# Where the first feed-forward block of a gated cross-attention kernel is normalized, quantized and transposed

## The chip, the cores and the metric

The kernel runs on one core of one Trainium2 chip. The metric is the device time of one execution in microseconds. A difference below about 0.3% (2.2 us here) can't be told from no change.

The core has five engines that each work through a queue of their own, in order: TensorE (PE; its weight loads are shown apart as PEld), VectorE (DVE), ScalarE (ACT), GpSimd (POOL) and SyncE (SP, which issues most of the DMA transfers). An engine stops at an instruction whose inputs aren't ready, and everything behind it in its queue stops too.

## The reference

4096 rows `x` of width 512 (two batches of 2048) go through a layer norm, 16-head attention over 77 context rows, a gated residual, a second layer norm, and a feed-forward net with per-tensor 8-bit quantization:

```
x = x + tanh(g_xattn) * attn(layernorm(x), ctx)        # 16 heads of 32, float32
h = layernorm(x)                                        # 4096 x 512
xq = round(h / sx),  sx = max|h| / 127                  # one scale for the whole tensor
h = gelu((xq @ w1q.T + b1) * sw1 * sx)                  # 4096 x 2048
hq = round(h / sh),  sh = max|h| / 127                  # one scale again
x = x + tanh(g_ffn) * ((hq @ w2q.T + b2) * sw2 * sh)
```

Each scale is a maximum over the whole tensor. Nothing of the first product can start before the last row of the attention is known, and nothing of the second before the last row of the GELU.

## The kernel before, in words

The rows are cut in 8 blocks (`i`) of 512 (`TB`), each held in SBUF as `X[i]`, four tiles (`t`) of 128 rows.

**Attention.** For every block there are eight steps `s` (head group `s // 2`, half of the rows `s % 2`), written out by hand. VectorE's and TensorE's orders are taken as written, where `tc.issue_after(ins)` queues an instruction behind `ins` on its engine and the other engines' orders come from a scheduler. A step holds a `softmax` (scores on TensorE, maximum and subtraction on VectorE, exponential on ScalarE, sum `sm` and reciprocal `rs` on VectorE, product with `rs` on GpSimd, line 282), the transposes `pta` of its result to `aT` (`transpose_a`), the product with the values (`apply_v`: `pc`, copied to `cT`) and the output projection of the block before (`project_o`, line 324, which adds to `X[i]`). `aT` has three buffers, `cT` seven. After its output projection a block gets the statistics of the second layer norm (`norm2_stats`: `mean2`, `rstd2`; the power that makes `rstd2` is a GpSimd instruction, line 142) and the block's largest absolute normalized value (`norm2_max`: `xf`, `tm`, `xmax`, lines 338 to 350). For the last block this is done tile by tile behind each `project_o(NB - 1, t)`.

**Between the stages.** `normalize_x(0, nc.gpsimd)` writes the normalized first block to `xs0` on GpSimd (line 520, four instructions), under a high priority and behind the last softmax product on GpSimd. `scale_of(xmax, "x", ...)` makes `m_x`, a TensorE product that spreads the maximum over the partitions (`pg_x`, line 153), and `s_x`, `inv_x`. `quantize_x(0, xs, 1)` quantizes the block tile by tile (VectorE for tiles 0 and 1, ScalarE and VectorE for 2 and 3), transposes each tile on TensorE (`px`, line 544) and copies it to `xqT` on ScalarE (line 547).

**First product.** For each block `i`, 128 matmuls of 128x512 (`ph`, line 574; eight of them fill one of two PSUM tiles), the GELU on ScalarE (line 581, two for each PSUM tile) into one of eight `G` buffers, a maximum of it on VectorE (`hmax`, line 591) and a store of `G` to DRAM (line 602). While block `i` is multiplied, block `i + 1` is prepared on VectorE: four normalizations (`xs`, line 520), two instructions that quantize the whole block (lines 164 and 165, to `xq`), and four copies (line 549) of the transposes `px` that TensorE makes between its matmuls. `xs`, `xq` and `xqT` have two buffers each (`fwork`), and `px` two PSUM buffers. In

```python
            if i + 1 < NB:
                with tc.issue_after(last):
                    xs = normalize_x(i + 1, nc.vector)
                xqT, last = quantize_x(i + 1, xs, NT)
```

`last` is the last quantizing instruction of the block before, and each block renews it. Within these bounds the scheduler picks the order.

**Second product.** Its scale needs the last `hmax`. The two last blocks' `G` are still in SBUF; the others are read back from DRAM.

Of the kernel before, what the change touches and what calls it, by code (L numbers as in the profile page):

```python
# [8 lines left out]
F32 = mybir.dt.float32  # L9
BF16 = mybir.dt.bfloat16  # L10
AF = mybir.ActivationFunctionType
ALU = mybir.AluOpType
# [3 lines left out]
P = 128  # L16
# [23 lines left out]
def tile_flamingo_gated_block(  # L40
# [47 lines left out]
    wq_sb = awts.tile([P, KC, D], F32, name="wq_sb")  # L88
    wo_sb = awts.tile([P, KC, D], F32, name="wo_sb")
    ctx_sb = awts.tile([P, B, KC, NK], F32, name="ctx_sb")  # L90
    bv_sb = awts.tile([NK, D], F32, name="bv_sb")
    bq_sb = const.tile([P, KC], F32, name="bq_sb")
    bk_sb = const.tile([P, KC], F32, name="bk_sb")
    tg = const.tile([P, 2], F32, name="tg")
    bo_sb = const.tile([P, D], F32, name="bo_sb")
    b1_sb = const.tile([P, FC], F32, name="b1_sb")
    b2_sb = const.tile([P, D], F32, name="b2_sb")

    load_x(0, pieces=NT)
    nc.scalar.dma_start(bq_sb, bq)  # L100
# [11 lines left out]
    nc.sync.dma_start(tg[:, 1:2], g_ffn.to_broadcast([P, 1]))  # L112
    nc.sync.dma_start(bo_sb, bo.to_broadcast([P, D]))
    nc.sync.dma_start(b1_sb, b1)
    nc.sync.dma_start(b2_sb, b2.to_broadcast([P, D]))

    ident = const.tile([P, P], F32, name="ident")
    make_identity(nc, ident)
# [5 lines left out]
    nc.gpsimd.memset(mhalf, -0.5)  # L124

    w1q = const.tile([P, KC, FF], BF16, name="w1q")
    w2q = const.tile([P, FC, D], BF16, name="w2q")
    mean2 = const.tile([P, NB, NT, 2], F32, name="mean2")
    rstd2 = const.tile([P, NB, NT], F32, name="rstd2")
# [15 lines left out]
    def scale_of(maxima, name, psum, tag):  # L145
# [13 lines left out]
        nc.vector.reciprocal(inv, s)  # L159
        return s, inv  # L160

    def quantize(dst, src, inv):

        nc.vector.tensor_scalar(src, src, inv, MAGIC, ALU.mult, ALU.add)
        return nc.vector.tensor_scalar(dst, src, MAGIC, None, ALU.subtract).ins
# [3 lines left out]

    s_w, inv_w = {}, {}  # L170
    with actx:
        work = actx.enter_context(tc.tile_pool(name="work", bufs=2))
        ps_s = actx.enter_context(tc.tile_pool(name="ps_s", bufs=2, space=PSUM))
        ps_t = actx.enter_context(tc.tile_pool(name="ps_t", bufs=2, space=PSUM))
        ps_p = actx.enter_context(tc.tile_pool(name="ps_p", bufs=2, space=PSUM))

        kblk, vblk = [], []
        for b in range(B):
            kb = awts.tile([P, NG, GK], F32, name=f"kb{b}")
            nc.gpsimd.memset(kb, 0.0)  # L180
            kblk.append(kb)
            vblk.append(awts.tile([NK, D], F32, name=f"vb{b}"))

        def project_k(b, g):

# [147 lines left out]
        def norm2_max(i, t0=0, t1=NT):  # L333

            tm = small.tile([P, NT], F32, tag="tm", name=f"tm{i}_{t0}")
            for t in range(t0, t1):
                xn = work.tile([P, D], F32, tag="xn", name=f"xf{i}_{t}")
                nc.vector.tensor_scalar(
                    xn,
                    X[i][:, t, :],  # L340
                    mean2[:, i, t, 0:1],
                    rstd2[:, i, t : t + 1],
                    ALU.subtract,
                    ALU.mult,
                )
                nc.vector.tensor_reduce(
                    tm[:, t - t0 : t - t0 + 1], xn, AX.X, ALU.max, apply_absolute_value=True
                )
            k = i if t1 - t0 == NT else NB - 1 + t0
            nc.vector.tensor_reduce(xmax[:, k : k + 1], tm[:, : t1 - t0], AX.X, ALU.max)  # L350

# [63 lines left out]
            project_k(0, 1)  # L417
        softmax(0, 0)
        for i in range(NB):
            for s in range(2 * NG):  # L420
                last = None
                if s + 1 < 2 * NG:
                    last = softmax(i, s + 1)
                    last_product = last["POOL"]
                elif i + 1 < NB:
                    last = softmax(i + 1, 0)
                transpose_a(i, s, 0)

                if i == 0 and s < 2:
                    project_k(0, s + 2)  # L430
                if s == 0:
                    if i > 0:
                        apply_v(i - 1, NG - 1)
                    project_q(i, 1)
                if i == 0 and s == 1:
                    project_v(0)
                if i == 0 and s == 2:


                    with tc.issue_after(last["ACT"]):  # L440
                        nc.scalar.activation(tg, tg, AF.Tanh)
                    with tc.issue_after(last["POOL"]):
                        nc.gpsimd.tensor_scalar(bo_sb, bo_sb, tg[:, 0:1], None, ALU.mult)
                if s in (2, 4):
                    project_q(i, 1 + s // 2)
                    apply_v(i, s // 2 - 1)
                if s in (1, 3, 5, 6) and i > 0:
                    project_o(i - 1, (1, 3, 5, 6).index(s))
                if s == 6:
                    apply_v(i, 2)  # L450
                if i + 1 < NB:
                    if s == 3:
                        with tc.issue_after(last["DVE"]):
                            norm(i + 1)
                    if s in (5, 6):
                        for t in (2 * s - 10, 2 * s - 9):
                            transpose_x(i + 1, t)
                transpose_a(i, s, 1)
                if s == 6 and i + 1 < NB:
                    project_q(i + 1, 0)  # L460
                if i == 0 and 3 <= s < 7:
                    for b in range(1, B):
                        project_k(b, s - 3)
                        if s == 6:
                            project_v(b)
                if s == 7 and i > 0:
                    norm2_stats(i - 1)
                    norm2_max(i - 1)
                if last is not None:
                    with tc.issue_after(last["DVE"]):  # L470
                        weight_step(i, s)
                    t = s - NT if i == 0 else s // 2
                    if t >= 0 and (i == 0 or s % 2 == 0):
                        with tc.issue_after(last["POOL"]):
                            add_bias(i, t)
            if i + 2 < NB:
                load_x(i + 2)
            if i == 0:
                load_w("w1", w1_piece, range(4))
            if i == 2:  # L480
                load_w("w2", w2_piece, range(2))
# [4 lines left out]
        for t in range(NT):  # L486
            project_o(NB - 1, t)
            last = norm2_stats(NB - 1, t, t + 1)
            if t > 0:
                with tc.issue_after(last):  # L490
                    norm2_max(NB - 1, t - 1, t)
        norm2_max(NB - 1, NT - 1, NT)
    s_w1, s_w2 = s_w["w1"], s_w["w2"]


# [1 line left out]
    hidden_dram = ctx.enter_context(  # L497
        tc.tile_pool(name="hidden_dram", bufs=1, space=bass.MemoryType.DRAM)
    )

    def gtile(name):
        return gpool.tile([P, GF, TB], F32, tag="G", name=name)
# [5 lines left out]
    with ExitStack() as fctx:  # L508
# [5 lines left out]
            tc.tile_pool(name="ps_x", bufs=2, space=PSUM, reuse_waits="tile")  # L514
        )

        def normalize_x(i, engine):
            xs = fwork.tile([P, NT, D], F32, tag="xs", name=f"xs{i}")
            for t in range(NT):
                engine.tensor_scalar(  # L520
                    xs[:, t, :],
                    X[i][:, t, :],
                    mean2[:, i, t, 0:1],
                    rstd2[:, i, t : t + 1],
                    ALU.subtract,
                    ALU.mult,
                )
            return xs

        def quantize_x(i, xs, n):  # L530

            xq = fwork.tile([P, NT, D], BF16, tag="xq", name=f"xq{i}")
            xqT = fwork.tile([P, KC, TB], BF16, tag="xqT", name=f"xqT{i}")
            for t0 in range(0, NT, n):
                v, vq = xs[:, t0 : t0 + n, :], xq[:, t0 : t0 + n, :]
                if n == 1 and t0 >= NT // 2:
                    nc.scalar.activation(v, v, AF.Copy, bias=MAGIC, scale=inv_x)
                    last = nc.vector.tensor_scalar(vq, v, MAGIC, None, ALU.subtract).ins
                else:
                    last = quantize(vq, v, inv_x)  # L540
                for t in range(t0, t0 + n):
                    px = ps_x.tile([P, KC, P], BF16, tag="px", name=f"px{i}_{t}")
                    for kc in range(KC):
                        nc.tensor.transpose(px[:, kc, :], xq[:, t, kc * P : (kc + 1) * P], identb)  # L544
                    dst = xqT[:, :, t * P : (t + 1) * P]
                    if n == 1:
                        nc.scalar.copy(dst, px)  # L547
                    else:
                        nc.vector.tensor_copy(dst, px)
            return xqT, last  # L550


        with tc.issue_after(last_product), tc.high_priority(offset=300):
            xs = normalize_x(0, nc.gpsimd)
        s_x, inv_x = scale_of(xmax, "x", ps_g, "pg")
        xqT, last = quantize_x(0, xs, 1)
        s1 = const.tile([P, 1], F32, name="s1")
        nc.vector.tensor_tensor(s1, s_x, s_w1, ALU.mult)
        b1s = const.tile([P, FC], F32, name="b1s")
        nc.vector.tensor_scalar(b1s, b1_sb, s1, None, ALU.mult)  # L560
        for i in range(NB):
            cur = xqT
            if i + 1 < NB:
                with tc.issue_after(last):
                    xs = normalize_x(i + 1, nc.vector)
                xqT, last = quantize_x(i + 1, xs, NT)
            for a in range(GT):
                G = gtile(f"G{i}_{a}")
                for v in range(GF // 2):
# [149 lines left out]
```

## Time and profile before

| | |
|---|---|
| median of 14 executions | 728.15 us (722.54 to 732.19) |
| the profiled execution: its time, its span | 730.5 us, 728.6 us |
| busy: PE, DVE, ACT, POOL | 672.2, 525.9, 346.0, 212.0 us |
| attention | 0 to 450.8 us |
| from the last `po` to the first `ph` | 450.8 to 467.3 us |
| first product | 467.3 to 596.0 us |
| second product | 600.9 us to the end |
| first product: PE busy, DVE busy | 127.4, 109.6 of 128.75 us |

The times are microseconds from the span's start. A row of the timeline gives the start, the time until the last of a merged group ended, the engine, the line of the kernel, the operation, the tile written and read, shapes, the count, and in brackets the engine's idle time just ahead and what ended it. The profile's busy time of PE contains modelled ends of matmuls, so a busy PE may still lose time.

### The profile page before, as it was taken

Reading aid. Unit: us, or ns where it says so; the run is one execution under the profiler, and the core shown is the slowest. Engines: PE = TensorE matmul, PEld = TensorE weight load, DVE = VectorE, ACT = ScalarE, POOL = GpSimd, SP = SyncE. Lnnn points to the kernel's source line nnn. Section 1 sums busy time; section 2 is a strip of 40 time slices with the busy share of each in tenths; the row PEclk is TensorE's granted clock in tenths of the full one; section 3 lists DMA queues with packets and bytes.
Section 4 is the critical chain, followed back from the end, with each engine's and each line's share of the span. In section 5 each row is a group of like instructions: output and inputs, shape, how many; then the busy total and the mean of one; then the engine's idle time right before and its main releaser. Section 6 shows DMA issues by size and latency. Waiting matters only on the chain.

```text
span 728.6 us, 7864 instructions
## 1 busy us (share of the span) xinstructions
PE 672.2 (92%) x2881; PEld 333.9 (46%) x2904; DVE 525.9 (72%) x821; ACT 346.0 (47%) x474; POOL 212.0 (29%) x164
## 2 busy tenths in 40 slices
PE   4998999899999999999999997499999978999977
PEld 2654545445445454554555543244444433444432
DVE  3564688879888889587577567699997769855442
ACT  1454444344343334444444441377777779454540
POOL 3223333234232342432333234100000009992000
PEclk9999999999999999999999999599999998999999
DMA  9801200021311311100000000057666107698861
GB/s 304 328 0 50 66 1 1 13 93 68 116 58 58 116 58 58 58 1 1 0 1 1 0 1 0 0 231 288 253 268 274 73 0 289 241 385 304 307 249 72
DMA packets 26430, 85.40 MB, mean 117 GB/s; under 512 B 3531, under 2 KB 3531, under 8 KB 20248
## 3 DMA queue, kind: packets, MB, share of 16 engines
q1 hardware_dynamic: 24520, 83.54, 30.9%
q10 hardware_dynamic: 1872, 1.37, 0.6%
q8 instruction: 23, 0.38, 0.2%
q14 instruction: 15, 0.12, 0.1%
HBM read 51.34 MB, written 33.55 MB: 117 GB/s over the span
## 4 chain that ended last, share of the span: by engine, by line
PE 66%; DVE 12%; DMA 7%; POOL 6%; ACT 6%; issue 2%; SPq 0%; POOLq 0%; DVEq 0%; ACTq 0%
PE ph L574 16%; PE pq L245 12%; PE po L317 11%; PE pf L636 8%; PE pta L295 7%; PE ps L261 6%; DMA Gb<-h 6%; POOL e L282 4%; PE pc L304 3%; DVE mx L270 2%; DVE sm L279 2%; ACT Gb L627 1%; DVE e L274 1%; POOL xs L520 1%; PE px L544 1%
## 5 line engine op out<-in xcount | busy, mean ns | idle before, releaser
L282 POOL TENSOR_TENSOR e<-e,rs 128x616 f32<-128x616 f32 x64 | 78.0, 1219 | 269.9 <-DVE rs L281 198.6
L574 PE MATMUL ph<-xqT,w1q 128*128 128x512 bf16 x499 | 124.0, 384 | 1.9 <-ACT xqT L547 0.7
L636 PE MATMUL pf<-w2q,hq 128*128 128x512 bf16 x502 | 114.7, 388 | 10.6 <-DVE hq L628 6.3
L245 PE MATMUL pq<-xnT,wq_sb 128*128 128x512 f32 x256 | 120.3, 609 | 0.9 <-ACT xnT L237 0.9
L296 ACT COPY aT<-pta 77x512 f32<-77x512 f32 x128 | 73.4, 580 | 98.6 <-PE pta L295 98.4
L317 PE MATMUL po<-wo_sb,cT 128*128 128x512 f32 x256 | 116.4, 593 | 0.0
L581 ACT ACTIVATE G<-ph,b1s,s 128x512 f32<-128x512 f32 x128 | 99.5, 777 | 30.1 <-PE ph L574 24.6
L650 POOL TENSOR_TENSOR x<-x,b_sb 128x512 f32<-128x512 f32 x32 | 58.9, 1879 | 142.2 <-DVE b_sb L607 142.2
L295 PEld LDWEIGHTS pta<-ident,e 128*77 128x77 f32 x512 | 60.3, 149 | 69.2 <-POOL e L282 34.0
L295 PE MATMUL pta<-ident,e 128*77 128x128 f32 x512 | 79.9, 282 | 12.3 <-POOL e L282 9.8
L591 DVE TENSOR_REDUCE hmax<-G 128x1 f32<-128x1024 f32 (+1 forms) x65 | 75.2, 1197 | 16.4 <-ACT G L581 16.1
L636 PEld LDWEIGHTS <-hq 128*128 128x128 bf16 x512 | 50.5, 99 | 74.5 <-issue 8.8
L270 DVE TENSOR_REDUCE mx<-ps 128x8 f32<-128x616 f32 x64 | 50.4, 788 | 44.8 <-PE ps L261 44.8
L574 PEld LDWEIGHTS <-w1q 128*128 128x128 bf16 x512 | 49.5, 98 | 68.5 <-issue 19.6
L261 PE MATMUL ps<-kb,qT 128*128 128x308 f32 x256 | 79.3, 430 | 0.5 <-ACT kb L200 0.4
L245 PEld LDWEIGHTS pq<-xnT,wq_sb 128*128 128x128 f32 x256 | 46.9, 194 | 52.7 <-issue 49.2
L627 ACT ACTIVATE Gb<-Gb,inv_h 128x2048 f32<-128x2048 f32 x24 | 47.6, 1999 | 47.8 <-DMA Gb<-h 47.8
L279 DVE TENSOR_REDUCE sm<-e 128x8 f32<-128x616 f32 x64 | 50.5, 789 | 26.8 <-ACT e L277 26.4
L277 ACT ACTIVATE e<-e 128x616 f32<-128x616 f32 x64 | 45.8, 716 | 50.0 <-DVE e L274 45.7
L317 PEld LDWEIGHTS po<-wo_sb,cT 128*128 128x128 f32 x256 | 46.4, 190 | 45.6 <-issue 43.9
L628 DVE TENSOR_SCALAR hq<-Gb 128x2048 bf16<-128x2048 f32 x24 | 36.5, 1531 | 32.9 <-ACT Gb L627 32.9
L274 DVE TENSOR_TENSOR e<-ps,mx 128x616 f32<-128x616 f32 x64 | 51.0, 796 | 3.3 <-POOL e L282 0.5
(90 smaller groups left out, 622.6 us busy)
## 6 DMA issues: line engine op xcount, KB each, us to landing
h<-G SPq DMA_DIRECT2D x24, 1024.0 KB, 3.9
Gb<-h SPq DMA_DIRECT2D x24, 1024.0 KB, 7.9
raw_w<-in_w2T SPq DMA_DIRECT2D x8, 1024.0 KB, 5.2
out_y<-x SPq DMA_DIRECT2D x32, 256.0 KB, 3.5
x<-in_x SPq DMA_DIRECT2D x7, 1024.0 KB, 5.3
raw_w<-in_w1T SPq DMA_DIRECT2D x4, 1024.0 KB, 10.0
x<-in_x SPq DMA_DIRECT2D x4, 256.0 KB, 5.5
wq_sb<-in_wqT ACTq DMA_DIRECT2D x1, 1024.0 KB, 10.2
```

Source lines behind the costliest of these rows:

```text
L245: nc.tensor.matmul(pq, wq_sb[:, kc, g * P : (g + 1) * P], xnT[i][:, kc, :], start=(kc == 0), stop=(kc == KC - 1),)
L261: nc.tensor.matmul(ps[:, u, :GK], qT[i, g][:, t * P : (t + 1) * P], kblk[i // NBB][:, g, :], start=True, stop=True,)
L270: nc.vector.tensor_reduce(mx, sc, AX.X, ALU.max)
L279: nc.vector.tensor_reduce(sm, e4, AX.X, ALU.add)
L282: last["POOL"] = nc.gpsimd.tensor_tensor(e4, e4, rs[:, :, :, None].to_broadcast([P, 2, HG, NK]), ALU.mult).ins
L295: nc.tensor.transpose(pt[:NK, j, :], es[i, s][:, u, j, :], ident)
L296: nc.scalar.copy(aT[i, g][:, :, t * P : (t + 1) * P], pt[:NK, :, :])
L317: nc.tensor.matmul(po, cT[i, g][:, t * P : (t + 1) * P], wo_sb[:, g, :], start=(g == 0), stop=(g == NG - 1),)
L574: nc.tensor.matmul(ph[:, u, :], w1q[:, kc, fc * P : (fc + 1) * P], cur[:, kc, :], start=(kc == 0), stop=(kc == KC - 1),)
L581: nc.scalar.activation(G[:, 2 * v + u, :], ph[:, u, :], AF.Gelu, bias=b1s[:, fc : fc + 1], scale=s1,)
L591: nc.vector.tensor_reduce(hmax[:, k + u : k + u + 1], G[:, 2 * v + u : 2 * v + u + n, :], AX.XY, ALU.max, apply_absolute_value=True,)
L636: nc.tensor.matmul(po[t], hq[:, fc, t * P : (t + 1) * P], w2q[:, fc, :], start=(fc == 0), stop=(fc == FC - 1),)
```

## The change

The first block's normalization moves to VectorE, into the last attention block: `normalize2(xs0[:, t, :], 0, t)` for four tiles, behind the last softmax's subtraction. `xs0` takes one of the three `aT` buffers, the quantized `xq0` takes the buffer of `xnT`, and the transposed block `xqT0` has a place of its own. `scale_of` and the first block's transposes use the attention's PSUM buffers, and the copies alternate between ScalarE and VectorE. The last tile's `norm2_max` is queued behind that of the tile before. `bv_sb` moves to a `cT` buffer, and `b2_sb` to a new pool `late`, so that its load is issued behind those of `x`. For blocks 1 to 7 the function `quantize_x(i)` holds the normalization too, all of it under one `tc.issue_after(last)`, and `last` stays what the first block left.

```diff
+    kblk = [awts.tile([P, NG, GK], F32, name=f"kb{b}") for b in range(B)]
+    vblk = [awts.tile([NK, D], F32, name=f"vb{b}") for b in range(B)]
+    work = actx.enter_context(tc.tile_pool(name="work", bufs=2))
+    bv_sb = work.tile([NK, D], F32, tag="cT", name="bv_sb", bufs=7)
-    bv_sb = awts.tile([NK, D], F32, name="bv_sb")
-    b2_sb = const.tile([P, D], F32, name="b2_sb")
-    nc.sync.dma_start(b2_sb, b2.to_broadcast([P, D]))
+    xqT0 = const.tile([P, KC, TB], BF16, name="xqT0")
...
+    def normalize2(dst, i, t):
+        nc.vector.tensor_scalar(
+            dst, X[i][:, t, :], mean2[:, i, t, 0:1], rstd2[:, i, t : t + 1],
+            ALU.subtract, ALU.mult,
+        )
+    def transpose_q(dst, src):
+        for kc in range(KC):
+            nc.tensor.transpose(dst[:, kc, :], src[:, kc * P : (kc + 1) * P], identb)
...
         for i in range(NB):
+            if i == NB - 1:
+                xs0 = work.tile([P, NT, D], F32, tag="aT", name="xs0", bufs=3)
             for s in range(2 * NG):
...
                 if last is not None:
                     with tc.issue_after(last["DVE"]):
                         weight_step(i, s)
+                        if i == NB - 1 and s == 6:
+                            for t in range(NT):
+                                normalize2(xs0[:, t, :], 0, t)
...
             if t > 0:
                 with tc.issue_after(last):
-                    norm2_max(NB - 1, t - 1, t)
-        norm2_max(NB - 1, NT - 1, NT)
+                    last = norm2_max(NB - 1, t - 1, t)
+        with tc.issue_after(last):
+            norm2_max(NB - 1, NT - 1, NT)
+        s_x, inv_x = scale_of(xmax, "x", ps_p, "pp")
+        xq0 = work.tile([P, NT, D], BF16, tag="xnT", name="xq0", bufs=1)
+        for t in range(NT):
+            v, vq = xs0[:, t, :], xq0[:, t, :]
+            if t < NT // 2:
+                with tc.issue_after(last):
+                    last = quantize(vq, v, inv_x)
+            else:
+                nc.scalar.activation(v, v, AF.Copy, bias=MAGIC, scale=inv_x)
+                last = nc.vector.tensor_scalar(vq, v, MAGIC, None, ALU.subtract).ins
+        for t in range(NT):
+            px = ps_t.tile([P, KC, P], BF16, tag="pt", name=f"px0_{t}")
+            transpose_q(px, xq0[:, t, :])
+            copy = nc.vector.tensor_copy if t % 2 else nc.scalar.copy
+            copy(xqT0[:, :, t * P : (t + 1) * P], px)
...
+    late = ctx.enter_context(tc.tile_pool(name="late", bufs=1, reuse_waits="tile"))
+    b2_sb = late.tile([P, D], F32, name="b2_sb")
+    nc.sync.dma_start(b2_sb, b2.to_broadcast([P, D]))
...
-        def normalize_x(i, engine):
-            xs = fwork.tile([P, NT, D], F32, tag="xs", name=f"xs{i}")
...
-        def quantize_x(i, xs, n):
+        def quantize_x(i):
+            xs = fwork.tile([P, NT, D], F32, tag="xs", name=f"xs{i}")
             xq = fwork.tile([P, NT, D], BF16, tag="xq", name=f"xq{i}")
             xqT = fwork.tile([P, KC, TB], BF16, tag="xqT", name=f"xqT{i}")
...
+            for t in range(NT):
+                normalize2(xs[:, t, :], i, t)
+            quantize(xq, xs, inv_x)
+            for t in range(NT):
+                px = ps_x.tile([P, KC, P], BF16, tag="px", name=f"px{i}_{t}")
+                transpose_q(px, xq[:, t, :])
+                nc.vector.tensor_copy(xqT[:, :, t * P : (t + 1) * P], px)
+            return xqT
...
-        with tc.issue_after(last_product), tc.high_priority(offset=300):
-            xs = normalize_x(0, nc.gpsimd)
-        s_x, inv_x = scale_of(xmax, "x", ps_g, "pg")
-        xqT, last = quantize_x(0, xs, 1)
...
         for i in range(NB):
-            cur = xqT
+            cur = xqT if i else xqT0
             if i + 1 < NB:
                 with tc.issue_after(last):
-                    xs = normalize_x(i + 1, nc.vector)
-                xqT, last = quantize_x(i + 1, xs, NT)
+                    xqT = quantize_x(i + 1)
```

## The prediction, made before the result was known

> **What bounds the kernel now.** I read the busy shares, then the chain that ended last, then the timeline around the place of the change. The chain runs through TensorE except at the seams between stages, and the first seam is the one that the change touches:
>
> ```profile
> 449.79 1.02 PE L317 MATMUL po<-wo_sb,cT 128*128 128x512 f32 x2
> 450.14 8.24 POOL L520 TENSOR_SCALAR xs<-x,mean,rstd 128x512 f32<-128x512 f32 x4
> 452.65 0.59 DVE L338 TENSOR_SCALAR xf<-x,mean,rstd 128x512 f32<-128x512 f32 x1
> 458.35 0.55 POOL L142 TENSOR_TENSOR rstd<-ve_f,mhalf 128x1 f32<-128x1 f32 x1
> 458.94 0.55 DVE L338 TENSOR_SCALAR xf<-x,mean,rstd 128x512 f32<-128x512 f32 x1 [5.70 <-POOL rstd L142]
> 460.89 0.17 DVE L149 TENSOR_REDUCE m_x<-xmax 128x1 f32<-128x11 f32 x1
> 461.44 0.79 PE L153 MATMUL pg_x<-diag_x,ones 128*128 128x128 f32 x2 [10.63 <-DVE diag_x L151]
> 467.28 0.59 PE L574 MATMUL ph<-xqT,w1q 128*128 128x512 bf16 x1 [0.67 <-ACT xqT L547]
> ```
>
> The last `rstd` is queued on GpSimd behind the four `xs` of the first block, VectorE waits 5.70 us for it, and TensorE stands 10.63 us. The next view is VectorE's timeline in the first product, and beside it the stretches with their clock (columns: stretch, its length, then busy time and count of PE, PEld, DVE, ACT, POOL, granted clock, DMA share, GB/s):
>
> ```profile
> 513.65 2.34 DVE L591 TENSOR_REDUCE hmax<-G 128x1 f32<-128x1024 f32 x2
> 515.91 1.45 DVE L520 TENSOR_SCALAR xs<-x,mean,rstd 128x512 f32<-128x512 f32 x3
> 517.36 2.34 DVE L591 TENSOR_REDUCE hmax<-G 128x1 f32<-128x1024 f32 x2
> 519.62 0.74 DVE L549 COPY xqT<-px 128x512 bf16<-128x512 bf16 x2
> 520.29 1.28 DVE L164 TENSOR_SCALAR xs<-xs,inv_x 128x2048 f32<-128x2048 f32 x1
> 521.48 0.75 DVE L549 COPY xqT<-px 128x512 bf16<-128x512 bf16 x2
> 522.14 2.34 DVE L591 TENSOR_REDUCE hmax<-G 128x1 f32<-128x1024 f32 x2
> 524.40 1.22 DVE L165 TENSOR_SCALAR xq<-xs 128x2048 bf16<-128x2048 f32 x1
> ```
> ```profile
> 452.00:456.00 4.00, 0.00 (x0) 0.00 (x0) 1.17 (x4) 0.00 (x0) 4.00 (x3) 0.95 0.00 0
> 456.00:460.00 4.00, 0.00 (x0) 0.00 (x0) 1.06 (x3) 0.00 (x0) 2.91 (x3) 0.50 0.00 0
> 472.00:473.00 1.00, 1.00 (x8) 0.51 (x7) 0.00 (x0) 0.40 (x1) 0.00 (x0) 0.67 0.00 0
> 510.00:520.00 10.00, 9.93 (x50) 4.41 (x50) 9.99 (x13) 8.04 (x11) 0.00 (x0) 1.00 0.62 256
> ```
>
> TensorE and VectorE are both full at 510 to 520: VectorE is no spare engine there. Its start-to-start steps are 1.13 us for an `hmax` (2.26 for two), 0.483 for an `xs`, 0.335 for a copy, 1.19 and 1.13 for the two quantizing instructions. The clock halves at about 455.6, 4.8 us after the last matmul, and is back at 472.66, 5.4 us after the first `ph`. TensorE's place in the same stretch is given by the transposes:
>
> ```profile
> 472.73 0.61 PE L544 MATMUL px<-identb,xq 128*128 128x128 bf16 x8
> 485.51 0.61 PE L544 MATMUL px<-identb,xq 128*128 128x128 bf16 x8
> 504.13 0.38 PE L544 MATMUL px<-identb,xq 128*128 128x128 bf16 x4
> 517.22 0.61 PE L544 MATMUL px<-identb,xq 128*128 128x128 bf16 x8
> ```
>
> **Part 1: the four GpSimd `xs` go.** The `rstd` would start at 452.8 and end by 453.6 (0.79 at 445.94, the longest of the single ones). It is no longer what VectorE waits for: `xf`, `tm`, `xmax` of tile 2 now stand ahead of tile 3's. From an `xf` start to its `xmax` end took 1.45 us at 449.22; twice that from 452.65, with 0.1 between, ends at 455.65. So `m_x` comes at 455.65 instead of 460.89: -5.24 us.
>
> **Part 2: four `xs` on VectorE in the last attention step.** Two stand between the last `e` (ends 430.03) and `sm`, one between `sm` and `rs`, one behind. The first two (0.97) partly cover the 0.78 that VectorE waits for the exponential; `rs` ends 0.75 later and the last softmax product on GpSimd at 433.98 instead of 433.23. TensorE first does `pc` and four other transposes until 433.7, so it waits 0.3; but the following `pta` wait for ScalarE's copy until 434.48 anyway, and the rest is under 0.1 at the last `pc` (435.81). The projection's `x` add behind them, 0.9 late, uses up VectorE's 1.13 and 0.45 idle at 435.6 and 440.5. Taken: +0.07; bounds -0.1 and +0.75 (the whole delay of `rs`).
>
> **Part 3: the seam's chain.** `m_x` to `inv_x` stays 2.05. Then before took 4.34 us to the first `ph`. After: `xs` 0.45, `b1s` 0.2, now ahead, `xq` 0.4, then tiles 1 to 3 in order until 2.7; the third and fourth tile wait for a free PSUM buffer, the fourth for VectorE's copy of the second (3.4); four transposes at half clock 0.6 and its copy 0.4 end at 4.4. +0.1. Sum of parts 1 to 3: **-5.1 us**, `ph` starts at 462.2 instead of 467.28; bounds -5.6 (`pg_x` and the transposes at full clock, 0.5 less) and -4.4 (part 2 at its 0.75).
>
> **Part 4: buffers and loads, no cost.** `aT` keeps two buffers in the last block; the one needed again was read two steps before. `xq0`'s and `pg_x`'s slots were last read by 420 and 449. `b2_sb`'s 256 KB leave the opening (19.35) and go on SP's queue behind the last `x`; it waits for `wq_sb`'s last reader, near 420. Queued behind it are the stores of `G`, the first at 474.8; its reader comes at 600. It landed in 6.2 us, which the 54 us until that store hide; uncovered it would cost those 6.2.
>
> **Part 5: the preparation of blocks 1 to 7.** The list of instructions of the built kernels shows what the frozen `last` does. Before, VectorE normalizes one block ahead, `hmax` in pairs. After, blocks 4 to 7 are normalized and quantized early, and the copies of block 3's transposes stand behind block 4's and most of block 5's preparation. Counted from the first copy of `px1` to the first copy of `px3`: before 16 `hmax`, 8 `xs`, 4 quantizing, 9 copies = 29.6 us (the trace has 30.8 with 0.87 idle: 1% over my steps). After: 15 `hmax` 16.95, 14 `xs` 6.76, 4 and 3 quantizing steps 8.15, 9 copies 3.02 = 34.9, with that 1% 35.2. To the first copy of `px4`: 22, 22, 6 and 4, 13: 51.5, or 52.0.
>
> Let S be the first `ph`. `px1` follows 23 matmuls instead of 13 (S+5.45 at 472.73): ten more at 0.216 and one 0.165 pause, S+7.75, its copy 0.42 later, S+8.2. VectorE then runs without a wait: first copy of `px3` done at S+43.4, of `px4` at S+60.2. TensorE needs them to free the PSUM buffers of the third tiles. Its queue has `px3_2` behind 140 matmuls; before it stood behind 138 at 504.13, S+36.85, so S+37.3 unhindered: **6.1 late**. `px4_2` is behind 196; before, `px4_0` was behind 192 at S+49.94; with four matmuls and eight transposes S+51.3: **8.9 late**. The delay builds as 0.6 and 0.9 at `px2`, 0.2 and 4.3 at `px3`, 2.8 at `px4`. After that VectorE has only `hmax`, a quantizing step and copies, 11.5 us from `px4` to `px5` (seven, one and four are between them), against 15.85 us per block on TensorE: nothing is given back, because from there TensorE is the bound. The last `hmax` and all of the second product move with it. Taken +8.9; bounds +7.0 and +10.5 (below). ScalarE isn't queued behind any of it: no `G` comes late.
>
> Lower bound: should the clock not fall at the seam, `px1` comes 2.6 earlier, but VectorE reaches it only 1.8 earlier: 7.1. Upper bound: a third of the 5 us that isolated durations (1.21, 0.54, 1.28, 1.22, 0.42) would add to the steps: 10.5.
>
> **A rule against the trace.** The rows give a clock fall after 4.8 idle us at 455.6, and one by 599 after 2.43 idle and 0.49 busy. The Trainium skill, "TensorE: Matmul & The Clock Gate", section "HAM oscillation — how this bites in real kernels", says to leave no idle gap of TensorE above about 3.4 us, which speaks against the new 4.3 us one. By the rule TensorE would then run 3.4 to 6.8 us at half speed, 1.7 to 3.4 lost; since it would wait 2.8 at `px4_2` in any case, the sum would be 4.4 at most by the rule, and is 3.8 by the rows, where 4.3 us is less than the 4.8 after which the clock fell. I take 3.8.
>
> **Sum.** -5.1 + 8.9 = +3.8. On the span 728.6 that gives 732.4; the profiled execution took 730.5 where the median is 728.15, and I move the median: **732.0 us**. Own range, extremes of both parts: -5.6 + 7.0 to -4.4 + 10.5, 729.5 to 734.3.
>
> **Rivals.**
> - *VectorE keeps up* (faster): TensorE finds `px3_2`'s buffer free, part 5 is 0, 728.15 - 5.1 = 723.1. It decides if the 34.9 us run takes under 28.8, the 15 `hmax` 0.73 each. Every paired row says 1.13, VectorE has no idle to give there. 0.10.
> - *The clock falls again in the stalls and stays low past `px4_2`*: the time that it took to come back after 467.28 (5.4 us), half lost (11 matmuls took 4.80 us from 468.09, eight take 1.73 at full clock): +2.7, 734.7. For: both falls above. Against: the last stall is 2.8 us and the earlier fall is eaten by it. 0.12.
> - *The clock stays up at the seam*: TensorE's gap shrinks from 10.6 to 5.3 us; part 5 loses 1.8: 730.2. Against: the fall at 599 after a shorter gap. 0.06.
> - *The change doesn't remove the wait* (another op ahead of `rstd` on GpSimd): nothing stands there in the list; within the first rival's tail.
>
> **How the numbers follow.** My forecast 0.72, nearly all of it above 730.3 (0.3% is what a measurement of this kernel can tell from no change). Slower: 0.68 + 0.12 = 0.80 and none of the rest in full; same: 0.04 + 0.06 = 0.10; faster 0.10. For 8 in 10 I leave out the first rival and the top of the second: 728.6 (0.9 under my own range, for the scatter of medians) to 735.2.
>
> **What would show it.** Right: the four `xs` on VectorE near 430, `m_x` some 5 us after the last `po`, PE idle of about 4 us ended by VectorE's copy near S+39 and about 3 near S+57, first product near 137.6 us instead of 128.75. Wrong: no PE idle over 1 us in the first product, or a delay that is made up before the last `hmax`.

## The result, and the profile after

| | before | after |
|---|---|---|
| median | 727.8 us (48 executions) | 758.46 us (10 executions) |
| the profiled execution: its time, its span | 730.5, 728.6 us | 759.06, 757.2 us |
| last `po` to first `ph` | 16.5 us | 11.1 us |
| first product (first to last `ph`) | 128.75 us | 164.4 us |
| last `ph` to the end | 132.6 us | 132.7 us |

The changed kernel takes 1.0421 times as long (95% interval 1.04 to 1.0443). The prediction had 732.0 us and at most 735.2; the time is far above that. It had the seam right, and the sign (slower) for a reason that is not the one found here.

The seam first. The timeline of the kernel after, around the last projection:

```profile
445.83 3.17 PE L329 MATMUL po<-wo_sb,cT 128*128 128x512 f32 x7
451.00 0.78 POOL L144 TENSOR_TENSOR rstd<-ve_f,mhalf 128x1 f32<-128x1 f32 x1 [2.66 <-DVE ve_f L143]
452.20 0.54 DVE L166 TENSOR_SCALAR xf<-x,mean,rstd 128x512 f32<-128x512 f32 x1
453.69 0.17 DVE L151 TENSOR_REDUCE m_x<-xmax 128x1 f32<-128x11 f32 x1
454.23 0.79 PE L155 MATMUL pg_x<-diag_x,ones 128*128 128x128 f32 x2 [5.23 <-DVE diag_x L153]
460.09 0.61 PE L579 MATMUL ph<-xqT,w1q 128*128 128x512 bf16 x1 [0.52 <-DVE xqT L520]
```

The `rstd` now starts as soon as its input is there, the `xf` behind it has no idle time, and TensorE waits 5.23 us for `diag_x` where it waited 10.63. The clock falls here all the same; the stretches of after (columns as in the prediction: the granted clock is the third number from the end):

```profile
452.00:454.00 2.00, 0.00 (x0) 0.00 (x0) 1.83 (x7) 0.00 (x0) 0.00 (x0) 0.90 0.00 0
454.00:455.00 1.00, 0.77 (x2) 0.50 (x2) 0.17 (x1) 0.00 (x0) 0.00 (x0) 0.50 0.00 0
462.00:464.00 2.00, 2.00 (x6) 0.70 (x5) 2.00 (x4) 1.06 (x2) 0.00 (x0) 0.54 0.00 0
464.00:466.00 2.00, 2.00 (x11) 0.79 (x9) 1.57 (x2) 1.66 (x3) 0.00 (x0) 1.00 0.00 0
```

A mean of 0.90 over the first 2 us is 0.4 us at 0.50: it is low from 453.6, 4.6 us after the last `po`, and full again from 463.8.

The loss is in the first product. TensorE's rows there, and the rows of VectorE's copies, in the timeline of after:

```profile
500.14 1.91 PE L579 MATMUL ph<-xqT,w1q 128*128 128x512 bf16 x8 [0.65 <-ACT G L586]
502.70 1.91 PE L579 MATMUL ph<-xqT,w1q 128*128 128x512 bf16 x8 [0.65 <-ACT G L586]
503.82 0.75 DVE L560 COPY xqT<-px 128x512 bf16<-128x512 bf16 x2
504.44 0.61 PE L177 MATMUL px<-identb,xq 128*128 128x128 bf16 x8
522.35 0.76 DVE L560 COPY xqT<-px 128x512 bf16<-128x512 bf16 x2 [0.53 <-PE ph L579]
522.83 0.38 PE L177 MATMUL px<-identb,xq 128*128 128x128 bf16 x4 [0.30 <-DVE xqT L560]
```

Eight matmuls start every 2.56 us, and ahead of each eight TensorE stands until a GELU (`G`) is done. The waits for VectorE's copies, which the prediction set at 4.3 us at `px3` and 2.8 at `px4`, are none and 0.30 us (1.2 us in the whole first product, in four waits of 0.30). The groups of the page say the same; of after, then of before:

```profile
L579 PE MATMUL ph<-xqT,w1q 128*128 128x512 bf16 x499 | 123.0, 381 | 34.4 <-ACT G L586 33.0
```
```profile
L574 PE MATMUL ph<-xqT,w1q 128*128 128x512 bf16 x499 | 124.0, 384 | 1.9 <-ACT xqT L547 0.7
```

The matmuls' busy time is nearly the same; 33.0 us of waits for `G` are new. They are most of the 164.4 - 128.75 = 35.7 us by which the first product is longer, and 35.7 less the seam's 5.4 makes +30.3, against +30.7 between the medians. (The two spans differ by 28.6 only: in the profiled execution of after, the attention ended at 449.0, where in the other runs' profiles it ended between 448.3 and 451.6.) The chain shows one period of it (columns: start, duration, what). After, from 501.85:

```profile
501.87 0.79 ACT G L586
502.66 0.04 issue
502.70 1.71 PE ph L579 x7
504.41 0.03 issue
```

0.79 + 0.04 + 1.71 + 0.03 = 2.57 us: one GELU and the eight matmuls stand one behind the other. Over the first product, GELUs are 28.7% of the chain of after. In the chain of before they are 4.3%, and for long stretches matmuls follow matmuls:

```profile
530.32 1.89 PE ph L574 x8
532.21 0.00 issue
```

What lets them stand one behind the other can't be read in either trace alone, since both name a PSUM tile only `ph`. The lists of instructions of the built kernels name the tile and its half. A PSUM tile holds two groups of four matmuls (call them n.0 and n.1 for tile n), each in a bank of its own and with a GELU of its own:

```
before         n.0 x4, (n+1).0 x4, n.1 x4, (n+1).1 x4, then the same for tiles n+2 and n+3
after          (n+1).0 x3, n.1 x4, (n+1).0 x1, then (n+2).0 x3, (n+1).1 x4, (n+2).0 x1
```

In both lists the first matmul of n.1 waits for the GELU of n.0: the tile is one object to the waits, though the two groups have different banks. Before, (n+1).0 lies between n.0 and n.1 and covers that GELU. After, n.1 ends one matmul ahead of (n+1).0, so the GELUs of n.1 and (n+1).0 become ready together; the next matmuls, (n+2).0, need the first of them and the group behind needs the second. The four matmuls that should cover a GELU have been done already.

### The profile page after: what moved, and what is told of

It is laid out like the page before. It is cut to its first block, busy times and chain, and to the rows that moved or that the text cites. A ratio compares the mean times of both kernels' runs of the same rounds, so it can differ in the third digit from the quotient of the medians.

```text
span 757.2 us, 7866 instructions
## 1 busy us (share of the span) xinstructions
PE 673.2 (89%) x2881; PEld 333.4 (44%) x2904; DVE 532.7 (70%) x827; ACT 338.5 (45%) x472; POOL 203.0 (27%) x160
## 4 chain that ended last, share of the span: by engine, by line
PE 58%; DVE 11%; ACT 10%; POOL 8%; DMA 8%; issue 3%; SPq 1%; another core or an unknown queue 0%; POOLq 0%; DVEq 0%; ACTq 0%
PE ph L579 14%; PE pq L257 12%; PE po L329 11%; PE pta L307 7%; DMA Gb<-h 7%; ACT G L586 6%; PE ps L273 6%; POOL x L655 4%; POOL e L294 4%; PE pc L316 3%; PE pf L641 2%; DVE mx L282 2%; ACT Gb L632 2%; DVE sm L291 1%; PE ptx L248 1%
## 5 line engine op out<-in xcount | busy, mean ns | idle before, releaser
L586 ACT ACTIVATE G<-ph,b1s,s 128x512 f32<-128x512 f32 x128 | 92.9, 773 | 73.1 <-PE ph L579 70.8
L596 DVE TENSOR_REDUCE hmax<-G 128x1 f32<-128x1024 f32 (+1 forms) x65 | 78.0, 1202 | 47.5 <-ACT G L586 47.1
L307 PEld LDWEIGHTS pta<-ident,e 128*77 128x77 f32 x512 | 59.9, 148 | 69.4 <-POOL e L294 34.7
```

The lines of the kernel that those rows point to most:

```text
L307: nc.tensor.transpose(pt[:NK, j, :], es[i, s][:, u, j, :], ident)
L586: nc.scalar.activation(G[:, 2 * v + u, :], ph[:, u, :], AF.Gelu, bias=b1s[:, fc : fc + 1], scale=s1,)
L596: nc.vector.tensor_reduce(hmax[:, k + u : k + u + 1], G[:, 2 * v + u : 2 * v + u + n, :], AX.XY, ALU.max, apply_absolute_value=True,)
```

## The experiments

Theory 1: the order of the matmuls over the PSUM tiles is the loss. Theory 2, the prediction's: VectorE's queue is. In the table are all runs; "1st product" and the waits are of each run's profiled execution.

| kernel | ratio to before (95%) | `po` to `ph` | 1st product | TensorE's waits for `G` |
|---|---|---|---|---|
| before | 1 | 16.5 | 128.75 | 0.2 |
| after | 1.0421 (1.04, 1.0443) | 11.1 | 164.4 | 33.0 |
| after, matmuls tied as before | 0.9916 (0.9879, 0.9952) | 11.1 | 127.8 | none |
| after, matmuls tied as written | 1.0667 (1.0613, 1.0721) | 11.1 | 181.0 | 51.1 |
| before, matmuls as after | 1.0535 (1.048, 1.059) | 16.5 | 166.7 | 34.7 |
| before, `last` frozen | 1.0551 (1.0491, 1.0611) | 16.5 | 165.6 | 32.6 |
| after, a tile for each group | 0.9846 (0.9805, 0.9887) | 11.1 | 122.0 | none |
| before, tied as it is | 1.0005 (0.9983, 1.0027) | 16.5 | 127.8 | 0.2 |
| after, loop of before | 1.0447 (1.0408, 1.0485) | 11.1 | 165.1 | 33.2 |
| after, tied as before, `last` renewed | 0.9934 (0.9909, 0.9959) | 11.1 | 128.1 | 0.8 |
| before, a tile for each group | 0.9912 (0.989, 0.9935) | 16.5 | 121.1 | none |
| after, a tile for each group, loop of before | 0.9834 (0.9799, 0.9869) | 11.1 | 121.2 | none |
| after, tied as before, VectorE's list kept | 1.0081 (1.0046, 1.0116) | 11.1 | 142.6 | 0.4 |

### The changed kernel with the order of before

```diff
-                for v in range(GF // 2):
-                    ph = ps_h.tile([P, 2, TB], F32, tag="ph", name=f"ph{i}_{a}_{v}")
-                    for u in range(2):
+                phs = [
+                    ps_h.tile([P, 2, TB], F32, tag="ph", name=f"ph{i}_{a}_{v}")
+                    for v in range(GF // 2)
+                ]
+                for u in range(2):
+                    for v in range(GF // 2):
+                        ph = phs[v]
...
-                            nc.tensor.matmul(
+                            with tc.issue_after(prev) if prev else ExitStack():
+                                prev = nc.tensor.matmul(
...
```

> The changed kernel, with the matmuls of the first product tied to each other in the order that the kernel before had (four of one PSUM tile, four of the other, in turn). Theory 1, the order of the matmuls: what costs the time is that TensorE now ends two groups of four back to back and then needs the PSUM tile that ScalarE has only just begun to read; eight matmuls take 2.56 us instead of 1.89. Then this kernel has 1.89 again, the first product is near 129 us instead of 164, and the time is that of before less the seam's 5.4 us: 721 to 725 us, 0.990 to 0.996 of before. Theory 2, VectorE: the preparation of blocks 1 to 7 comes too late in VectorE's queue, whatever order the matmuls have: the time stays above 745 us, with TensorE waiting for VectorE's copies.

Measured: 721.6 us against 727.85, 0.9916. The order of the matmuls alone turns a loss of 4.2% into a gain of 0.8%. One reservation: with the matmuls tied, the scheduler also listed VectorE's instructions differently (block 3's copies stand ahead of block 4's quantization again), so this run doesn't show what the changed kernel's own list on VectorE would cost. The last experiment does.

### The changed kernel, tied in the order of the source

The same tie (`issue_after(prev)` around each matmul), with the loops as they are written: n.0, n.1, (n+1).0, (n+1).1.

> The changed kernel, with the matmuls of the first product tied in the order of the code (eight of one PSUM tile, then eight of the next). Theory 1: ScalarE is never the last to be waited for, eight matmuls take 1.73 us; now TensorE is quick enough to meet the late copies in VectorE's queue that the prediction counted: waits of 2 to 6 us for VectorE ahead of the transposes of blocks 2 and 3, some 10 us in all, and a time of 719 to 727 us. Theory 2: above 745 us. If the prediction's count of VectorE's queue was wrong too, there are no such waits and the time is near 713 us.

Measured: 775.31 us, 1.0667. This is not what theory 1 expected in its first form, which held that two groups of one tile, one behind the other, would do. Theory 2 had the time (above 745 us), but not the wait: TensorE waits 51.1 us for `G` and not once for VectorE's copies of blocks 1 to 7. The chain of this run:

```profile
532.52 1.90 PE ph L581 x8
534.42 0.03 issue
534.44 0.79 ACT G L588
535.23 0.04 issue
```

A whole GELU stands in each period of 2.75 us. That brought up the wait inside the tile: n.1 waits for n.0's GELU with nothing between them to cover it.

### Before, with the order of after; and before, with `last` frozen

```diff
...
+                    this = (i, a, v, G, ph, cur)
+                    multiply(this, 0, range(KC - 1))
+                    if held_back:
+                        multiply(held_back, 1, range(KC))
+                        gelu(held_back, 1)
+                        finish(held_back)
+                    multiply(this, 0, [KC - 1])
+                    gelu(this, 0)
+                    held_back = this
...
```

> The kernel before, with nothing changed but the order of the matmuls in the first product: tied to the order that the changed kernel got (three of the next PSUM tile's first half, four of the current one's second half, one of the next one's first half). Theory 1: 2.56 us for eight matmuls, TensorE waits about 0.65 us for ScalarE some 60 times; 755 to 765 us, 1.037 to 1.05 of before. Theory 2: VectorE's work is that of before, so 726 to 735 us.

```diff
-                xqT, last = quantize_x(i + 1, xs, NT)
+                    xqT, _ = quantize_x(i + 1, xs, NT)
```

> The kernel before, with nothing changed but the loop's ordering: the normalization and the quantizing of a block both behind the last quantizing step of the first block, which is not renewed. The seam is as before. The built program shows the matmuls in the changed kernel's order from the twentieth on. Theory 1: eight matmuls in 2.56 us, 752 to 764 us. Theory 2: TensorE waits for VectorE's copies, 737 us (8.9 us, the prediction's count) or more, with eight matmuls in 1.89 us between these waits.

Measured: 765.55 us (1.0535) and 766.71 us (1.0551). The waits of the one, then of the other:

```profile
PE ph L569 <- ACT G L581: 34.7, 57, 1.3
```
```profile
PE ph L574 <- ACT G L581: 32.6, 52, 1.3
```

The order costs 37.7 us where nothing else was edited; both runs lie a little above theory 1's ranges (755 to 765 and 752 to 764 us). In the first of them the scheduler also put block 3's copies behind block 4's quantization on VectorE, but TensorE's waits for VectorE's copies are 1.8 us in all there, against the 34.7 for `G`. And the second run needs no tie: `last` frozen is enough for the scheduler to list the matmuls that way.

### A PSUM tile for each group

```diff
-            tc.tile_pool(name="ps_h", bufs=2, space=PSUM, reuse_waits="tile")
+            tc.tile_pool(name="ps_h", bufs=4, space=PSUM, reuse_waits="tile")
...
-                    ph = ps_h.tile([P, 2, TB], F32, tag="ph", name=f"ph{i}_{a}_{v}")
                     for u in range(2):
+                        ph = ps_h.tile([P, TB], F32, tag="ph", name=f"ph{i}_{a}_{v}{u}")
...
```

> The changed kernel, with one thing altered: each group of four matmuls writes a PSUM tile of its own (one bank, four of them) where before two groups shared a tile of two banks (two of them). The PSUM taken, the work and the number of matmuls stay; they are issued group after group, as in the run whose matmuls were tied as written (775.3 us). Theory 1a (in that run the second group of a tile waits for the GELU of the first group of the same tile, since the tile is one object to the waits; 1.89 us of matmuls + 0.87 us of that wait = 2.75 us): without the shared tile there is no such wait; the TensorE waits for G are under 3 us in all, eight matmuls take 1.89 us, and the time is 719 to 725 us. Theory 1b (what costs is that two groups for one tile end next to each other, so that ScalarE gets its work in pairs, whoever owns the bank): 31 to 51 us of waits for G remain and the time is 755 to 775 us. Theory 2 (VectorE's late copies): 732 us.

Measured: 714.8 us, 0.9846. The order of the matmuls is that of the run tied as written, group behind group, and the PSUM taken is the same; the unit of the wait is smaller, and 60 us are gone. (The scheduler also listed VectorE's instructions and the transposes a little differently in the two; neither run has more than 0.7 us of waits for VectorE's copies.) Theory 1a holds and 1b falls. But it is faster than 1a expected (719 to 725). The group, and a stretch, of this run:

```profile
L579 PE MATMUL ph<-xqT,w1q 128*128 128x512 bf16 x499 | 115.1, 384 | 1.4 <-DVE xqT L520 0.5 <-issue 0.2
```
```profile
520.00:540.00 20.00, 19.43 (x109) 9.49 (x109) 20.00 (x27) 15.78 (x21) 0.00 (x0) 1.00 0.68 279
```

The same 499 recorded matmuls are busy for 115.1 us, where before's are for 124.0: with pipelined matmuls a short wait for a GELU lies inside "busy". It shows in the weight loads. TensorE's weight loads in before's timeline, with a pair of GELUs between them, and then the loads in this run's:

```profile
511.71 1.61 PEld L574 LDWEIGHTS <-w1q 128*128 128x128 bf16 x8 [0.28 <-issue]
512.77 1.64 ACT L581 ACTIVATE G<-ph,b1s,s 128x512 f32<-128x512 f32 x2 [0.25 <-PE ph L574]
513.60 1.61 PEld L574 LDWEIGHTS <-w1q 128*128 128x128 bf16 x8 [0.28 <-issue]
```
```profile
528.97 8.08 PEld L579 LDWEIGHTS <-w1q 128*128 128x128 bf16 x38
```

Before has a gap of 0.28 us in every eight, and the loads go on at 513.60, 0.05 us after the first GELU of the pair ends (512.77 + 0.78); the divided tiles give 38 loads in a row. In this run VectorE is busy for all of 520 to 540, and TensorE for 19.43 of these 20 us: both are full there.

The Trainium skill, "Perfetto Trace Analysis", section "Optimizing Tensor Performance", wants independent groups of matmuls to go to different PSUM banks, so that emptying one overlaps the next group. All these kernels do that, with four banks in turn; the runs add that it isn't enough where the waits are kept by a tile of two banks (775.3 us, against 714.8 with a tile for each).

### Controls: before with the tie; the seam alone; `last` renewed

The kernel before with its own order tied:

> The kernel before, with its matmuls tied to the alternating order that it has anyway (four of one tile, four of the next, then the second fours). A control for the run of the changed kernel with the same ties (721.6 us): theory 1 (the order of the matmuls is the whole of the loss, the rest of the change is a gain at the seam): 726 to 730 us, so that the two tied kernels differ by the seam's 5 to 7 us. If the ties by themselves gave something: 722 or less, and the seam's gain would not be shown by the times.

The changed kernel with the loop as before:

```diff
                 with tc.issue_after(last):
-                    xqT = quantize_x(i + 1)
+                    xs = normalize_x(i + 1)
+                xqT, last = quantize_x(i + 1, xs)
...
```

> The changed kernel, with the loop as before (the next block's four normalizations alone are held back behind the last quantization, and that marker is renewed for each block): only the seam's part of the change is left. In the built program its matmuls still come as three of the next tile, four of this one, one of the next, as in the changed kernel. Theory 1 (that order costs 33 to 38 us, whatever led the scheduler to it): 754 to 762 us, with 30 us or more of TensorE's waits for G. Theory 2 (the marker that is no longer renewed makes VectorE late, and that is the loss): 719 to 725 us.

The changed kernel, tied as before, with `xqT, last = quantize_x(i + 1)`:

> The changed kernel with the matmuls tied to the alternating order (721.6 us with the marker frozen) and, besides, the marker renewed for each block, so that the whole of the next quantization is held back behind the one before. What the frozen marker costs by itself, with TensorE at 1.89 us per eight matmuls. Theory 1 (nothing: VectorE's copies come in time either way): 719 to 724 us, within 0.4% of the run with the marker frozen. Theory 2 (the prediction's 8.9 us are there, and the tied run hid them): 711 to 716 us.

Measured: 727.3 us (1.0005), 759.1 us (1.0447) and 721.37 us (0.9934). The tie by itself gives nothing, so the tied pair differs by the seam: 721.6 against 727.3, -5.7 us. (These two ran on different chips; 721.37 and 727.3 ran on one chip and differ by 5.9.) The loop of before doesn't help the changed kernel, since its list still has the costly order: the waits of that run,

```profile
PE ph L582 <- ACT G L589: 33.2, 54, 1.3
```

So the order tips with either half of the change, the frozen `last` alone or the seam alone. Why the scheduler picks it was not settled. The third run is within 0.2% of the tied one with `last` frozen. In both, the scheduler listed block 3's copies ahead of block 4's quantization, so this pair can't show what late copies would cost.

### The divided tile in the kernel before, and with the loop of before

> The kernel before, with the PSUM tile of two groups divided into one tile for each group of four matmuls (four tiles of one bank). In the changed kernel that division gave 714.8 us where the tied alternating order gave 721.6 us: ScalarE's GELUs then run close together and matmuls start every 0.22 us where they had started every 0.236 us. Theory 1 (before, too, loses the same 6 to 8 us in short waits of a tile's second group for its first GELU, inside what the profile counts as busy): 718 to 723 us, and the first product of the feed-forward part takes 120 to 124 us where it took 128.75 us. Theory 1c (before has no such waits, and the gain belongs to the changed kernel's order): 726 to 729 us.

> The changed kernel with one tile for each group and, besides, the loop as before (the next block's normalizations alone held back, the marker renewed). VectorE was busy all of 480 to 540 us in the run with one tile for each group (20.00 of every 20 us), so that what the frozen marker costs should show here if it ever does. Theory 1 (it costs nothing: the work on VectorE is the same, only its order differs, and TensorE's waits for VectorE's copies were 1.4 us): 712 to 717 us, within 0.4% of 714.8 us. Theory 2 (part of the prediction's 8.9 us is there once TensorE is quick): 705 to 711 us.

Measured: 719.68 us (0.9912) and 713.29 us (0.9834). Before, too, lost 6.9 us (726.55 - 719.68) in waits that the profile counts as busy; theory 1c falls. With divided tiles the seam is worth 719.68 - 713.29 = 6.4 us. The second run is the fastest version of all, though not apart from the one with `last` frozen (0.9834 and 0.9846, with overlapping intervals).

### What VectorE's list costs where TensorE isn't held up

Both lists are written out. Every VectorE instruction of the first product is tied behind the one before it, in the changed kernel's own order; TensorE's matmuls are tied in the order of before.

```diff
...
+        def tied(engine, emit):
+            with tc.issue_after(last[engine]) if last[engine] else ExitStack():
+                last[engine] = emit().ins
...
+                w = dve.pop(0)
+                tied("DVE", lambda: vector(w))
...
```

> The changed kernel with both lists written out: VectorE's instructions of the first product in the changed kernel's own order (the copies of block 3's transposes behind block 4's and most of block 5's preparation), TensorE's matmuls in the order of before (alternating), the transposes behind the same number of matmuls as in the changed kernel. This is the case that the prediction's part 5 worked out, and that neither the changed kernel (TensorE slow) nor the tied run (721.6 us, whose VectorE list came out differently) shows. Theory 2 (part 5's term is right where TensorE is not held up): TensorE stands some 4 us near its first product's start + 39 us and some 3 us near + 57, the time is 721.6 + 8.9 = 730.5 us (728.6 to 732.1). Theory 1 alone (VectorE's list costs nothing in any case): 721 to 724 us.

Measured: 735.6 us against 727.35, 14.0 us above the run tied as before. (The ratio in the table is 1.0081 where the medians give 1.0113: two of the seven executions took 731.4 and 731.7 us, five 735.5 to 736.5. By the table's ratios the distance from the tied run is 1.65%, 12 us.) TensorE's waits, and its timeline, in this run:

```profile
PE px L602 <- DVE xqT L622: 8.8, 6, 3.9
PE px L602 <- DVE xq L618: 0.8, 1, 0.8
```
```profile
477.90 0.62 PE L602 MATMUL px<-identb,xq 128*128 128x128 bf16 x8 [0.78 <-DVE xq L618]
480.94 0.71 PE L602 MATMUL px<-identb,xq 128*128 128x128 bf16 x8 [0.69 <-DVE xqT L622]
489.47 9.46 PE L577 MATMUL ph<-xqT,w1q 128*128 128x512 bf16 x39
502.82 1.01 PE L602 MATMUL px<-identb,xq 128*128 128x128 bf16 x8 [3.89 <-DVE xqT L622]
521.90 0.94 PE L602 MATMUL px<-identb,xq 128*128 128x128 bf16 x8 [2.30 <-DVE xqT L622]
```

Part 5's stalls are there. From the first `ph` at 460.59 they end at +42.2 and +61.3 us, with 3.89 and 2.30 us (predicted 4.3 and 2.8), and 0.78 and 0.69 at `px2` (0.6 and 0.9). Three more of 0.56 to 0.78 follow, which part 5 didn't have. Together 9.6 us. The rest is the clock; the stretches of the same run:

```profile
498.90:502.80 3.90, 0.03 (x1) 0.00 (x0) 3.90 (x6) 0.78 (x1) 0.00 (x0) 0.87 0.36 143
502.80:504.00 1.20, 1.18 (x9) 0.94 (x9) 1.20 (x4) 0.00 (x0) 0.00 (x0) 0.50 0.00 0
508.00:509.00 1.00, 0.84 (x4) 0.38 (x4) 0.59 (x2) 0.06 (x1) 0.00 (x0) 0.69 0.97 393
519.60:521.90 2.30, 0.00 (x0) 0.00 (x0) 2.30 (x4) 0.78 (x1) 0.00 (x0) 1.00 0.69 285
521.90:523.00 1.10, 1.10 (x9) 0.76 (x9) 1.10 (x2) 0.00 (x0) 0.00 (x0) 0.67 0.88 358
525.00:526.00 1.00, 1.00 (x6) 0.41 (x5) 0.10 (x1) 0.36 (x1) 0.00 (x0) 0.66 0.00 0
```

A mean of 0.87 over 3.9 us is 1.0 us at half clock, so it falls at 501.8 and comes back at 508.6: 5.8 us of work at half speed, 2.9 lost. The second time it falls near 522.3, after TensorE has begun again, and is back at 525.7: 1.7 lost. 9.6 + 2.9 + 1.7 = 14.2, where the first product is 142.6 - 127.8 = 14.8 us longer. Theory 2 holds in this kernel, and its size was put too low: the stalls alone are 9.6 us where it had 8.9, and the clock adds 4.6. In the changed kernel the same list on VectorE costs 1.2 us of waits, since there TensorE comes about as late as VectorE's copies.

## Why the prediction was right or wrong

**Parts 1 to 3, the seam: right.** Predicted -5.1 us from the last `po` to the first `ph`, measured -5.4 in the traces, and -5.7 and -6.4 between the medians of the two pairs that have the same order of matmuls. `m_x` comes 4.7 us after the last `po`, as "some 5 us" said. Of part 2, the four `xs` stand where they were put (428.2 to 430.9), TensorE waits 0.29 us for the softmax product behind them (0.3 predicted), and from the last `pc` to the last `po` both kernels take 15.0 us.

**Part 4, buffers and loads: right.** The load of `b2_sb` is issued at 418.49 ("near 420"), ahead of the first store of `G` at 466.41, and from the last `ph` to the end after takes 132.7 us where before took 132.6.

**Part 5: wrong, in the words "S+37.3 unhindered".** The step counted how many matmuls `px3_2` is queued behind, 140, and took their pace from before, where eight take 1.89 us; in the changed kernel they take 2.56. It did not look at which PSUM tile each of the 140 belongs to. In the changed list `px3_2` comes at 504.44, S+44.35, and `px4_2` at S+62.7 where the step had S+51.3. The term that was left out, TensorE's waits for `G`, is 33.0 of the 35.7 us by which the first product is longer, about four times the 8.9 us that were put in. So the forecast "slower" came true by luck: the VectorE stalls that it was added up from shrink to 1.2 us in the changed kernel, and without them the prediction's sum was -5.1. Running the changed kernel's list with before's order of matmuls (735.6 us) and running before with the changed order (765.55 us) separate the two.

**VectorE's half of part 5: right, and covered.** Its first copy of `px3` was predicted done at S+43.4, with no wait of VectorE ahead of it. After has it at 503.82 + 0.42, S+44.15, with 1.3 us of VectorE's waits on the way, and 0.2 us before TensorE's transposes that need it; the last experiment has it at S+42.2, without such a wait. At `px4` the roles are the other way round: VectorE itself waits 0.53 us, for a matmul. "ScalarE isn't queued behind any of it: no `G` comes late" is true of VectorE's queue, but the wait that did come is for `G`.

**The rule against the trace: decided wrongly.** This had no part in the miss, since the stall of 4.3 us doesn't occur in the changed kernel. The prediction saw that the clock had fallen 4.8 us after the last matmul, and took the stall of 4.3 us to stay under it. Where that stall occurred, at 3.89 us, the clock had fallen 2.9 us after the last matmul, and the loss of 2.9 us lies in the 1.7 to 3.4 that the prediction estimated from the Trainium skill, "TensorE: Matmul & The Clock Gate", section "HAM oscillation — how this bites in real kernels". The rule's limit of about 3.4 us isn't a safe one either: the second fall followed a gap of 2.30 us. The one row of 4.8 us was no lower bound, and another row of the same trace (2.43 us at 599) had said so. Nor was the earlier fall "eaten" by the stall at `px4`, as the prediction had it: VectorE was held up by the late TensorE too (2.40 us for a `G` at 510.99), and that stall still took 2.30 us.

**The rivals.** *VectorE keeps up* gave 723.1. In the changed kernel VectorE does keep up, but only because TensorE is slow; the tied kernel, where TensorE isn't, takes 721.6. *The clock falls again* gave +2.7 and is what the last experiment shows, with +4.6. *The clock stays up at the seam* is refuted by the 0.50 at 454. No rival had ScalarE or the PSUM tiles in it, and the range, built from rivals on VectorE and the clock, could not hold the result.

## What to carry to other kernels

Where a scheduler orders the matmuls, compare for each matmul which PSUM tile it writes and whose reading it waits for, before and after the change; a count of instructions ahead of it is not a pace. Where the waits are kept by the tile, make a PSUM tile as large as one group that is read by one instruction: with two groups in one tile the second waited for the reading of the first. Dividing the tile, which let the matmuls go group behind group, took 0.9% off a kernel that seemed full (0.9912); in the changed kernel it took away all 4.2% of the loss and left the gain of the seam (0.9846). A busy share of TensorE near 100% hid such waits here (127.4 of 128.75 us in before); a regular gap in the weight loads gave them away.

## What the runs showed of the hardware that was not expected

- The time from TensorE's last matmul to the fall of its clock was 4.8 us (before, 455.6), 4.6 us (after, 453.6), 2.9 us (501.8 in the last experiment) and 2.7 us (522.3, there with 0.4 us of transposes in it). It came back 3.8 us after the first `ph` (463.8) in after and 5.4 us in before. Worked out in the same way for the seam of all 13 profiled executions, the fall came 2.3 us after the last `po` (before with a tile for each group: `po` ends at 448.27, mean clock 0.78 from 450 to 451) up to 5.3 us after it (after with the loop of before: 451.22, 0.74 from 456 to 457). A single observation is no bound.
- 128x512 bf16 matmuls start every 0.236 us on average (eight in 1.89) with the shared tile and every 0.216 us without it (38 weight loads in 8.08 us, the last of them about 0.1 long, so 37 steps in 7.98), at the same mean duration for one, 384 ns, in the groups. The duration of one says nothing about the pace.
